# A fixed order at the tokenizer's end, Wv transposed earlier, and gathers that wait for an earlier unit

## The chip, the cores and the metric

The kernel runs on one core of a Trainium2 chip. A core has five engines with instruction streams of their own: TensorE (PE; its weight loads are listed as PEld), VectorE (DVE), ScalarE (ACT), GpSimd (POOL) and SyncE (SP). Each executes its stream in order and meets the others at semaphores. Transfers go through 16 DMA engines; they are issued by SP, ACT or, for gathers and scatters by a list of rows, by GpSimd. The metric is the device time of one execution, in microseconds. All data are 32-bit floats.

## The reference

Four images of 3 x 224 x 224 go through a tower of two layers:

- The tokenizer cuts each image into 28 x 28 = 784 patches of 8 x 8 x 3 = 192 numbers, normalises each, multiplies by W1 (to 256), normalises, multiplies by Wp1, normalises, applies SiLU and multiplies by Wp2. The reference repeats the tokens three times (`concatenate([q, k, tokens])`); the kernel computes them once (3136 rows of 256 in all) and writes the result three times.
- Layer 0: h is normalised twice (once ahead of the block, once in it), projected to queries, keys, values and a gate; the attention is over the four images, not over the tokens; then Wo, and h is added. After it a mixture of 6 experts of three matrices each, the best two per row.
- Layer 1: a linear attention (`qkv = x @ W_qkv`; q and k centred and squared, with k^T v per image), then Wout, and h added; after it a shared network and 4 small experts, the best two per row.

## The kernel before

Rows are handled in 28 tiles of 112, seven to an image. Up to the experts of layer 0 and in the last stage they go in 7 groups of 4 tiles (`groups`, `GT = 4`); in layer 1's attention in 8 units, two to an image, of 4 and 3 tiles (`units`, L1400).

The framework derives semaphores from the tiles that each instruction reads and writes. Inside `tc.manual_schedule(engines=...)` the named engines keep the order of the program; elsewhere a planner sets the order of each engine by its own modelled times. Either way, an engine that waits holds up all that stands behind it in its stream.

**Tokenizer (L506 to L573).** `first_rows(g)` multiplies a group's patches (`pw`, L515), takes statistics (L519), the root (L523) and its reciprocal, scales and adds (`y`, L528), takes statistics again (L531), a second root (L534) and writes the normalised rows `xn` (L538). `turned_rows` transposes them on PE and applies SiLU on ACT (L548). The last part multiplies by Wp2 (`pwp`) and adds into `h` (L566). `tokenize(g)` does the first part of group g, the second of g-1 and the third of g-2; the loop over g = 0 to 6 is in the planner's hands.

**Keys and values (L1049 to L1104), written out by hand.** `second_norm(g)` and `second_rows(g)` normalise h twice (statistics L236, roots L239 and L245, rows L1060). `keys_values(g)` transposes the rows, applies gamma and beta (`mT`, L1070), and multiplies by Wk and Wv (`pkv`, copied at L1079); the normalisation of group g+1 stands in between. The leftover parts of the tokenizer, `tokenize(7)` and `tokenize(8)`, stand around `keys_values(0)`:

```python
second_rows(0, second_norm(0))
tokenize(len(groups))
keys_values(0)
tokenize(len(groups) + 1)
for g in range(1, len(groups)):
    keys_values(g)
```

**Zero fill (L468 to L481).** Two tables in HBM, `xrows` and `yrows`, of 20224 rows each, are filled with zeros from the tile `nothing`, by SP, once `cols` is there. The experts' input rows are scattered into `xrows` (L950) and their results land in `yrows` (L1250).

**Experts of layer 0 (L1257 to L1512).** 30 blocks of 256 rows. At their end `fetch(u)` (L1411) gathers a unit's two result rows per token, by two indirect DMAs per tile (L1420) into `ys`, of which there are three; `fetch(0)`, `fetch(1)` and `fetch(2)` stand here, each behind the blocks that may hold its rows.

**Layer 1's attention (L1599 to L1805), in the planner's hands.** For a unit u: `stats_one` adds the gathered rows into h with their weights (L1434) and takes statistics; `normalise` writes `xa` (L1457); `x_t` transposes; `q_k` multiplies to q and k (`pqk`, L1625), adds the bias on DVE (L1629), squares and sums on ACT (L1633, L1634), and calls `stats_one` of unit u+1; `scales` makes the reciprocals and `uk` (L1657, ACT), `fold` sums. For each image `k_x` (`pukx`, L1699), `g_t` and `kv_out` make a matrix from `uk`, and `rows_out` writes h. `layer1_weights`, in unit 1, transposes Wv (L647), copies it (L651), multiplies by Wout (`pwvo`, L656). `fetch(3)` is called at the head of unit 0, and `fetch(u + 3)` at the head of each later unit:

```python
if u == 0:
    fetch(3)
    x_t(1)
    q_k(0, 0, GT)
```

Of the kernel before, what the change touches and what calls it, by code (L numbers as in the profile page):

```python
# [60 lines left out]
def tile_vit_tower(ctx: ExitStack, tc: tile.TileContext, a: dict, out: bass.AP):  # L61
# [230 lines left out]
    def halves(tiles):  # L292
        return [tiles[i : i + 2] for i in range(0, len(tiles), 2)]
# [3 lines left out]
    def cut(t0, n):  # L297
        return slice(t0 * TT, (t0 + n) * TT)
# [168 lines left out]

    nothing = tokp.tile([P, 8 * D], F32, tag="nothing", name="nothing")  # L468
    nc.gpsimd.memset(nothing, 0.0)
    for r in range(0, XROWS, 8 * P):  # L470
        n = min(8, (XROWS - r) // P)
        for rows_ in (xrows, yrows):
            put = nc.sync.dma_start(
                out=rows_[r : r + n * P, :].rearrange("(p k) d -> p (k d)", k=n),
                in_=nothing[:, : n * D],
            )
            tc.add_manual_dep(
                put.ins, turned.ins.name,
                mybir.DependencyInfo(mybir.DependencyClass.Sync, mybir.DependencyReason.DATA),
                reason="later",  # L480
            )  # L481
# [23 lines left out]

    def first_rows(g):  # L506

        t0 = groups[g][0]
# [14 lines left out]
        nc.scalar.activation(r, r, AF.Sqrt, bias=zero[:TT])  # L523
        nc.vector.reciprocal(r, r)
        st = small.tile([TT, GT, 6], F32, tag="st", name="st")
        mv = small.tile([TT, GT, 2], F32, tag="mv", name="mv")
        for j in range(GT):
            nc.vector.scalar_tensor_tensor(  # L528
                y[:, j, :], y[:, j, :], r[:, j : j + 1], bp1, ALU.mult, ALU.add
            )  # L530
            nc.vector.bn_stats(st[:, j, :], y[:, j, :])  # L531
            nc.vector.bn_aggr(mv[:, j, :], st[:, j, :])
        r = small.tile([TT, GT], F32, tag="rstd", name="rstd")
        nc.scalar.activation(r, mv[:, :, 1], AF.Sqrt, bias=eps[:TT])  # L534
        nc.vector.reciprocal(r, r)
        xn = tokw.tile([TT, GT, D], F32, tag="xn", name="xn")
        for j in range(GT):
# [3 lines left out]
            )  # L541
        return xn

# [13 lines left out]
    def tokenize(g):  # L557
        if g < len(groups):
            normed[g] = first_rows(g)
        if 1 <= g <= len(groups):  # L560
            third[g - 1] = turned_rows(normed.pop(g - 1))
        if g >= 2:
            sT = third.pop(g - 2)
            t2 = groups[g - 2][0]
            for two in halves(range(GT)):
                nc.vector.tensor_tensor(  # L566
                    h[:, t2 + two[0] : t2 + two[0] + 2, :],
                    mm_rows(two, lambda c, j: sT[:, c, cut(j, 1)], Wp2, "pwp2"),
                    over(bp2, 2), ALU.add,
                )  # L570
    for g in range(len(groups)):
        tokenize(g)
    tok.close()  # L573
    tcol = const.tile([NQ, 4], F32, tag="tcol", name="tcol")
# [66 lines left out]

    def layer1_weights():
        WvT = w1p.tile([P, 2, D], F32, tag="WvT", name="WvT")
        pt = ps_tile("pwv").rearrange("p (k i) -> p k i", k=2)
        for k in range(2):
            for c in range(2):
# [3 lines left out]
                )  # L650
        nc.vector.tensor_copy(WvT, pt)  # L651
        Wvo = w1p.tile([P, 2, D], F32, tag="Wvo", name="Wvo")
        for c in range(2):
# [36 lines left out]
    nc.vector.tensor_scalar(bgh, col2("bg"), 0.5, None, ALU.mult)  # L690
    ENG = mybir.EngineType
    by_hand = {ENG.DVE, ENG.PE, ENG.Activation}
    qTs, gates, atts, oTs, sums, rows0, turned0, logits0, picked, mixed = ({} for _ in range(10))
# [354 lines left out]

    xns = {}  # L1049

    def second_norm(g):
        t0 = groups[g][0]
        return ln_stats(lambda j: h[:, t0 + j, :], GT, twice=True)

    def second_rows(g, stats):
        mv, r = stats
        t0 = groups[g][0]
        xn = xns[g] = tokw.tile([TT, GT, D], F32, tag="xn", name="xn")
        for j in range(GT):
            nc.vector.tensor_scalar(  # L1060
                xn[:, j, :], h[:, t0 + j, :], mv[:, j, 0:1], r[:, j : j + 1],
                ALU.subtract, ALU.mult,
            )

    def keys_values(g):
        t0 = groups[g][0]
        at = cut(t0, GT)

        def put(c, pt):
            nc.scalar.activation(  # L1070
                mT[:, c, at], pt, AF.Identity, scale=col("gamma", c), bias=col("beta", c)
            )

        transposed(xns.pop(g), GT, put)
        if g + 1 < len(groups):
            stats = second_norm(g + 1)
        for w, dst in ((Wk, kT), (Wv, vT)):
            for o in range(2):
                nc.scalar.copy(  # L1079
                    dst[:, o, at],  # L1080
                    mm_t(GN, w, slice(o * P, (o + 1) * P), lambda c: mT[:, c, at], "pkv"),
                )
            if dst is kT and g + 1 < len(groups):
                second_rows(g + 1, stats)

        ht = h[:, t0 : t0 + GT, :]
        nc.vector.tensor_tensor(ht, ht, over(bo, GT), ALU.add)

    with tc.manual_schedule(engines=by_hand):
        second_rows(0, second_norm(0))  # L1090
        tokenize(len(groups))
        keys_values(0)
        tokenize(len(groups) + 1)
        for g in range(1, len(groups)):
            keys_values(g)

            if g == 1:
                for o in range(2):
                    q_mm(0, o)
                    q_copy(0, o)  # L1100
            t, rest = divmod((g + 1) * GT, TPI)
            if rest < GT and g + 1 < len(groups):
                for o in range(2):
                    products(0, o, [t - 1])  # L1104
# [306 lines left out]
    def fetch(u):  # L1411
# [5 lines left out]
        for j in range(n):  # L1417
            for k in range(2):
# [4 lines left out]
                )  # L1423
                tc.add_to_no_dep_group("fetched", got.ins)

    lw = []

# [214 lines left out]
    def scales(u):  # L1642
# [13 lines left out]
        for j in range(n):  # L1656
            nc.scalar.activation(uk[:, j, :], qk[:, j, D:], AF.Copy, scale=ss[:, j, 1:2])  # L1657
            nc.vector.tensor_scalar(
                qk[:, j, :D], qk[:, j, :D], ss[:, j, 0:1], None, ALU.mult
            )  # L1660
        for j in range(n):
            nc.scalar.activation(sq[:, j, :], uk[:, j, :], AF.Square)
# [93 lines left out]
    for u in range(len(units) + 2):  # L1756
        b, odd = divmod(u - 2, 2)
        one_image = u >= 2 and not odd
        if u == 0:
            fetch(3)  # L1760
            x_t(1)
            q_k(0, 0, GT)
            squares[0] = scales(0)
            fold(0, squares.pop(0))
            continue
        if u < len(units):
            fetch(u + 3)
        if u == len(units):
# [13 lines left out]
        if u < len(units):  # L1782
            q_k(u, 2, GT)
            if u == 1:
                lw.extend(layer1_weights())
                Wvo, bvo = lw[:2]
            squares[u] = scales(u)
        if one_image and b:
            kv_out(b, gT)
# [113 lines left out]
```

## Time and profile before

| | |
|---|---|
| median of 4 runs | 824.34 us (822.27 to 830.22) |
| profiled execution | 821.9 us, its span 820.0 us, mean granted clock 0.952 |
| PE busy | 738.7 us, 90% |
| DVE busy | 501.3 us, 61% |
| ACT busy | 333.6 us, 41% |
| POOL busy | 131.9 us, 16% |
| DMA | 97.38 MB; about 420 GB/s from 40 to 130 us, under 330 after that |

The profile is of one execution; times count from its first instruction. A row of the timeline gives start, duration, engine, line, operation, what is written from what is read, and how many; in brackets the engine's idle time before it, and what ended it. "issue" means that nothing the profile shows was waited for, "remote" that a semaphore ended the wait whose raising the profile can't put down to an instruction. A row x16 is 16 records; PE shows two records for each multiplication of 32-bit floats. In the page's slices each digit is a tenth of a slice (20.5 us). "PEclk" is the granted clock of PE in tenths of full speed. Matrix tiles in PSUM have names with p (`pqk`), numbers at a name's end are left out.

From the timeline, layer 1's units begin (first `pqk`) at 489.6, 496.4, 556.9, 564.8, 584.1, 600.6, 619.9 and 636.4 us.

### The profile page before, as it was taken

Reading aid. Unit: us, or ns where it says so; the run is one execution under the profiler, and the core shown is the slowest. Engines: PE = TensorE matmul, PEld = TensorE weight load, DVE = VectorE, ACT = ScalarE, POOL = GpSimd, SP = SyncE. Lnnn points to the kernel's source line nnn. Section 1 sums busy time; section 2 is a strip of 40 time slices with the busy share of each in tenths; the row PEclk is TensorE's granted clock in tenths of the full one; section 3 lists DMA queues with packets and bytes.
Section 4 is the critical chain, followed back from the end, with each engine's and each line's share of the span. In section 5 each row is a group of like instructions: output and inputs, shape, how many; then the busy total and the mean of one; then the engine's idle time right before and its main releaser. Section 6 shows DMA issues by size and latency. Waiting matters only on the chain. (4 is left out here: it accounts for less than half of the span.)

```text
span 820.0 us, 10856 instructions
## 1 busy us (share of the span) xinstructions
PE 738.7 (90%) x3516; PEld 501.1 (61%) x3516; DVE 501.3 (61%) x1549; ACT 333.6 (41%) x789; POOL 131.9 (16%) x219
## 2 busy tenths in 40 slices
PE   6899969999898787999999996189999999999996
PEld 4755545556565565888888873165777675555553
DVE  4677765769778743355447565179994745554441
ACT  0557754455574651432223225026554503222221
POOL 5200000000165236300120206542000000000000
PEclk9999979999999887999999998679999999999998
DMA  8499996000021944332342343211000003333333
GB/s 199 128 420 417 421 419 265 1 1 0 6 73 46 321 143 128 113 100 92 97 132 86 117 119 91 79 48 31 1 1 1 1 4 77 103 94 94 92 95 93
DMA packets 58182, 97.38 MB, mean 119 GB/s; under 512 B 14519, under 2 KB 48494, under 8 KB 53262
## 3 DMA queue, kind: packets, MB, share of 16 engines
q1 hardware_dynamic: 50832, 80.52, 28.4%
q0 software_dynamic: 6112, 14.01, 5.9%
q10 hardware_dynamic: 1182, 2.16, 1.1%
q8 instruction: 28, 0.46, 0.2%
q14 instruction: 28, 0.23, 0.1%
HBM read 30.93 MB, written 65.74 MB: 118 GB/s over the span
## 5 line engine op out<-in xcount | busy, mean ns | idle before, releaser
L950 POOL DMA_INDIRECT xrows<-xn,pos x56 | 59.6, 1064 | 255.2 <-ACT kq L714 206.5
L1420 POOL DMA_INDIRECT ys<-yrows,pos x56 | 54.5, 974 | 161.2 <-DMA yrows<-yb 132.4
L1224 PE MATMUL pb<-xTb,own 128*128 128x256 f32 x240 | 59.6, 393 | 5.9 <-issue 2.3
L1241 PE MATMUL pyb<-own,hb 128*128 128x256 f32 x240 | 58.7, 387 | 3.8 <-ACT hb L1230 3.8
L1230 ACT ACTIVATE hb<-pb,own 128x256 f32<-128x256 f32 x74 | 34.8, 474 | 61.1 <-PE pb L1224 40.6
L1224 PE MATMUL pb<-hb,own 128*128 128x256 f32 x240 | 58.8, 389 | 0.3 <-DVE hb L1232 0.3
L1224 PEld LDWEIGHTS pb<-xTb,own 128*128 128x128 f32 x240 | 45.3, 197 | 15.5 <-issue 4.2
L1241 PEld LDWEIGHTS pyb<-own,hb 128*128 128x128 f32 x240 | 46.0, 193 | 11.3 <-ACT hb L1230 5.0
L1625 PE MATMUL pqk<-Wqkv,lxT 128*112 128x512 f32 x112 | 49.7, 594 | 0.5 <-ACT lxT L81 0.5
L515 PE MATMUL pw<-Wall,pT 128*112 128x512 f32 x112 | 49.3, 593 | 0.0
L1224 PEld LDWEIGHTS pb<-hb,own 128*128 128x128 f32 x240 | 44.5, 195 | 6.3 <-DVE hb L1232 0.9
L1214 ACT COPY xTb<-ptb 128x512 f32<-128x512 f32 x30 | 17.5, 584 | 71.9 <-PE ptb L1210 59.5
L1247 DVE TENSOR_TENSOR yb<-pyb,eb 128x512 f32<-128x512 f32 x30 | 20.7, 691 | 41.9 <-PE pyb L1241 35.7
L1699 PE MATMUL pukx<-xa,uk 112*128 112x258 f32 x112 | 28.6, 411 | 18.7 <-ACT uk L1657 18.7
L264 PE MATMUL pt<-ident,xn 112*128 112x112 f32 x224 | 35.1, 291 | 11.2 <-DVE xn L538 6.6
L273 PE MATMUL pe<-xT,eW 128*128 128x448 f32 x112 | 45.2, 546 | 0.0
L264 PEld LDWEIGHTS pt<-ident,xn 112*128 112x128 f32 x224 | 27.5, 154 | 25.2 <-issue 8.8
L1232 DVE TENSOR_SCALAR hb<-pb,own 128x256 f32<-128x256 f32 x46 | 22.1, 481 | 31.4 <-PE pb L1224 27.6
L1699 PEld LDWEIGHTS pukx<-xa,uk 112*128 112x128 f32 x112 | 22.4, 206 | 22.4 <-issue 19.1
L515 PEld LDWEIGHTS pw<-Wall,pT 128*112 128x112 f32 x112 | 19.6, 177 | 25.1 <-issue 21.4
L739 DVE SCALAR_TENSOR_TENSOR prod<-kq 128x784 f32<-128x784 f32 x32 | 30.3, 969 | 7.1 <-ACT kq L714 5.2
L1625 PEld LDWEIGHTS pqk<-Wqkv,lxT 128*112 128x112 f32 x112 | 19.3, 177 | 24.8 <-issue 23.0
(361 smaller groups left out, 1497.2 us busy)
## 6 DMA issues: line engine op xcount, KB each, us to landing
xrows<-nothing SPq DMA_DIRECT2D x19, 1024.0 KB, 19.6
yrows<-nothing SPq DMA_DIRECT2D x19, 1024.0 KB
out_dram<-h SPq DMA_DIRECT2D x26, 336.0 KB, 3.8
xb<-xrows SPq DMA_DIRECT2D x30, 256.0 KB, 2.7
yrows<-yb SPq DMA_DIRECT2D x30, 256.0 KB, 2.1
ew<-in_L_ffn_expert_w_dram SPq DMA_DIRECT2D x6, 768.0 KB, 11.8
wb<-wd SPq DMA_DIRECT2D x28, 112.0 KB, 3.0
img<-in_x_dram SPq DMA_DIRECT2D x2, 588.0 KB
```

Source lines behind the costliest of these rows:

```text
L264: nc.tensor.transpose(pt[:, j * TT : (j + 1) * TT], xn[:, j, c * P : (c + 1) * P], ident[:TT, :TT])
L273: nc.tensor.matmul(pm[: wcols.stop - wcols.start, :n], w[:, c, wcols], xT(c), start=(c == 0), stop=(c == chunks - 1),)
L515: nc.tensor.matmul(pm, pTf[:, c, cut(t0 + j, 1)], Wall[:, c, :], start=(c == 0), stop=(c == 1))
L739: nc.vector.scalar_tensor_tensor(prod, qTs[s][:, o, :], 1.0, kT[:, o, t * SEQ : (t + 1) * SEQ], ALU.mult, ALU.mult, accum_out=atts[s][:, o ...
L950: put = nc.gpsimd.indirect_dma_start(out=xrows[:, :], out_offset=bass.IndirectOffsetOnAxis(ap=pos[:, k, t0 + j : t0 + j + 1], axis=0), in_ ...
L1224: nc.tensor.matmul(pm, wm[:, c, o * P : (o + 1) * P], src[:, c, :], start=(c == 0), stop=(c == 1),)
L1230: nc.scalar.activation(dst[:, o, :], pm, AF.Relu, bias=b)
L1232: nc.vector.tensor_scalar(dst[:, o, :], pm, b, 0.0, ALU.add, ALU.max)
L1241: nc.tensor.matmul(pm[:, t, :], src[:, c, t * P : (t + 1) * P], wm[:, c, :], start=(c == 0), stop=(c == 1),)
L1420: got = nc.gpsimd.indirect_dma_start(out=y[:, j, k, :], out_offset=None, in_=yrows[:, :], in_offset=bass.IndirectOffsetOnAxis(ap=pos[:, k, ...
L1625: nc.tensor.matmul(pqk, xT[:, c, cut(j, 1)], Wqkv[:, c, : 2 * D], start=(c == 0), stop=(c == 1),)
L1699: nc.tensor.matmul(pg, uks[u][:, k, c * P : (c + 1) * P], xas[u % 4][:, k, : D + 2], start=(j == 0), stop=(j == TPI - 1),)
```

## The change

Four edits:

1. In the tokenizer, `first_rows` is cut into three steps (`first_steps`, a generator). The loop ends with group 5; the last group is written out by hand, its three steps with the turning of group 5 and the last part of group 4 between them. The second normalisation of group 0 is moved ahead of group 5. In the keys, each group's transposes go one group ahead (`turn_second(g + 1)` between Wk and Wv of g) and its normalisation two groups ahead; `xn` gets three buffers, and the tokenizer's remaining parts stand inside `keys_values(0)`.
2. The zero tile `nothing` is 7 rows wide in place of 8, so the fill has 23 DMAs for each table in place of 20.
3. The transposes of Wv and their copy (`turn_wv`) are called in unit 0, ahead of its `pqk`, in place of unit 1.
4. `fetch(3)` is taken out of unit 0, and each unit calls `fetch(u + 2)` behind `scales(u)` in place of `fetch(u + 3)` at its head. From unit 3 on each gather waits for the last `uk` of the unit two before.

```diff
-    nothing = tokp.tile([P, 8 * D], F32, tag="nothing", name="nothing")
+    nothing = tokp.tile([P, 7 * D], F32, tag="nothing", name="nothing")
...
-    for r in range(0, XROWS, 8 * P):
-        n = min(8, (XROWS - r) // P)
+    for r in range(0, XROWS, 7 * P):
+        n = min(7, (XROWS - r) // P)
...
     def first_rows(g):
+        for _ in first_steps(g):
+            pass
+
+    def first_steps(g):
...
         nc.vector.reciprocal(r, r)
+        yield
         st = small.tile([TT, GT, 6], F32, tag="st", name="st")
...
             nc.vector.bn_aggr(mv[:, j, :], st[:, j, :])
+        yield
         r = small.tile([TT, GT], F32, tag="rstd", name="rstd")
...
-    for g in range(len(groups)):
+    n = len(groups)
+    for g in range(n - 1):
+        if g == n - 2:
+            second_rows(0, second_norm(0))
         tokenize(g)
+    ENG = mybir.EngineType
+    by_hand = {ENG.DVE, ENG.PE, ENG.Activation}
+    with tc.manual_schedule(engines=by_hand):
+        steps = first_steps(n - 1)
+        next(steps)
+        third[n - 2] = turned_rows(normed.pop(n - 2))
+        next(steps)
+        last_rows(n - 3)
+        for _ in steps:
+            pass
     tok.close()
...
+    def keys_values(g):
+        projected(g, Wk, kT)
+        if g + 2 < len(groups):
+            stats = second_norm(g + 2)
+        if g == 0:
+            third[n - 1] = turned_rows(normed.pop(n - 1))
+        turn_second(g + 1)
+        projected(g, Wv, vT)
+        if g == 0:
+            last_rows(n - 1)
+        if g + 2 < len(groups):
+            second_rows(g + 2, stats)
...
     with tc.manual_schedule(engines=by_hand):
-        second_rows(0, second_norm(0))
-        tokenize(len(groups))
+        turn_second(0)
+        last_rows(n - 2)
+        second_rows(1, second_norm(1))
         keys_values(0)
-        tokenize(len(groups) + 1)
         for g in range(1, len(groups)):
             keys_values(g)
...
                 tc.add_to_no_dep_group("fetched", got.ins)
+                if u >= 3:
+                    tc.add_manual_dep(
+                        got.ins, scaled[u - 2],
+                        mybir.DependencyInfo(
+                            mybir.DependencyClass.Sync, mybir.DependencyReason.DATA
+                        ),
+                        reason="paced",
+                    )
...
         for j in range(n):
-            nc.scalar.activation(uk[:, j, :], qk[:, j, D:], AF.Copy, scale=ss[:, j, 1:2])
+            got = nc.scalar.activation(uk[:, j, :], qk[:, j, D:], AF.Copy, scale=ss[:, j, 1:2])
...
+        scaled[u] = got.ins.name
...
         if u == 0:
-            fetch(3)
             x_t(1)
+            WvT = turn_wv()
             q_k(0, 0, GT)
...
-        if u < len(units):
-            fetch(u + 3)
...
             if u == 1:
-                lw.extend(layer1_weights())
+                lw.extend(layer1_weights(WvT))
                 Wvo, bvo = lw[:2]
             squares[u] = scales(u)
+            fetch(u + 2)
```

`last_rows(g)` is the third part of `tokenize`, `turn_second(g)` the transposes and `mT` of `keys_values`, and `projected(g, w, dst)` one of its two products, each with its code unchanged. In the tokenizer and in `second_rows` the tile `xn` is asked for with `bufs=3`.

## The prediction

> **What bounds the kernel now.** I read the slices of the page first, for where TensorE (PE) is not full.
>
> ```profile
> ## 2 busy tenths in 40 slices
> PE   6899969999898787999999996189999999999996
> ...
> DVE  4677765769778743355447565179994745554441
> ...
> PEclk9999979999999887999999998679999999999998
> ```
>
> A slice is 20.5 us. From slice 27 (about 555 us) on PE is full to the end, so whatever brings that point forward shortens the kernel. Before it, two slices stand out that the change touches: slice 5 (102 to 123, the tokenizer's end) and slices 24 to 26 (492 to 553, the border of the layers), where DVE, ACT and PE are all low in slice 25. Next I read PE's timeline for the first hole:
>
> ```profile
> 101.96 0.59 PE L284 MATMUL pwp<-Wp,xTt 128*112 128x256 f32 x2
> 102.39 0.74 PE L264 MATMUL pt<-ident,xn 112*128 112x112 f32 x6
> 102.97 3.19 PE L284 MATMUL pwp<-Wp,xTt 128*112 128x256 f32 x14
> ...
> 112.97 2.08 PE L264 MATMUL pt<-ident,xn 112*128 112x112 f32 x8 [6.57 <-DVE xn L538]
> 114.83 5.88 PE L284 MATMUL pwp<-Wp,xTt 128*112 128x256 f32 x16
> 120.55 0.93 PE L264 MATMUL pt<-ident,xn 112*128 112x112 f32 x8
> 121.92 3.27 PE L273 MATMUL pkv<-mT,Wk 128*128 128x448 f32 x8 [0.43 <-ACT mT L1070]
> ```
>
> PE waits 6.57 us for the last group's normalised rows, and then runs at half speed: eight transposes take 2.08 us, where the same eight take 0.93 at 120.55; the granted clock is 0.50 from 110 to 115. Then the waits of the second hole (who waited, for whom, us, times, longest):
>
> ```profile
> PE pukx L1699 <- ACT uk L1657: 18.7, 1, 18.7
> ...
> ACT lqT L81 <- remote: 11.1, 1, 11.1
> DVE ss L1648 <- remote: 8.5, 1, 8.5
> ...
> ACT junk L1634 <- remote: 6.0, 2, 4.3
> DVE lqT L83 <- remote: 5.9, 1, 5.9
> ACT s L1649 <- remote: 5.6, 1, 5.6
> ```
>
> "remote" is a semaphore raised late by nothing that the profile shows. DVE's `ss` at 517.77 needed ACT's sum that ended at 515.5 at the latest; `lqT` at 533.21 needed PE transposes that ended at 513.8. Last, GpSimd's timeline for what runs beside it:
>
> ```profile
> 493.98 0.92 POOL L1420 DMA_INDIRECT ys<-yrows,pos  x1 [22.19 <-DMA yrows<-yb]
> 495.21 0.93 POOL L1420 DMA_INDIRECT ys<-yrows,pos  x1 [0.30 <-issue]
> ...
> 527.65 0.93 POOL L1420 DMA_INDIRECT ys<-yrows,pos  x1 [0.30 <-issue]
> 537.67 0.92 POOL L1420 DMA_INDIRECT ys<-yrows,pos  x1 [9.09 <-DVE h L1434]
> ```
>
> 28 gathers run back to back from 494.0 to 528.6 (units 2 to 5, one each 1.24 us). All late semaphores of the kernel lie in such runs or just behind them: up to 2.1 us behind the 8 gathers ending at 417.2, 7.3 us in the 14 scatters of 297.8 to 315.5, and 509 to 533 here. Two runs of 14 scatters, at 1.42 and 1.44 us each, and five of 6 or 8 show none. I take the run of gathers as the cause; that it is one is inferred.
>
> **The change, part by part.** Times are against the profiled execution: 821.9 us, span 820.0 and 1.9 around it. The median of the runs shown, 824.34, is 2.4 above.
>
> *Paced gathers.* `fetch(3)` leaves unit 0 and comes after `scales(1)`; each later `fetch(u)` waits for the last `uk` of unit u-2. GpSimd has only gathers queued there, so the wait holds up nothing else. The run of 28 ends after 8, at 503.8, before the first late semaphore (509). Without these ACT goes on: its last square of unit 1 starts at 509.0 in place of 514.98 (without the 1.6 waited at 509.34 and the 4.3 ahead of it) and ends at 509.6. In unit 0 it took 2.0 from there (501.58) to the first `uk` (503.59), so unit 1's `uk` starts at 511.6. Before it started at 533.64 and unit 2's first `pqk` at 556.9, 23.3 later. I keep the 23.3 (PE waits some 4 us for `uk` then too, so its slow clock stays): `pqk` of unit 2 at 534.9, **22.0 us earlier**; 0 if the semaphores stay late.
>
> What is late next: the gathers. Unit 2's `uk` took 12.8 us from its first `pqk`, so ends at 547.7. `fetch(4)` takes 8 x 1.24 = 9.9, its last pair is used 2.65 after issue (493.98 to 496.63), less 0.9 of issue already counted: 11.7. Then two multiply-adds, statistics and mean (1.5), root, reciprocal and four rows (2.5), eight transposes and a copy (1.5): `pqk` of unit 4 at 564.9. Before it came 27.2 behind unit 2's (584.1 and 556.9), so at 562.1: **2.8 us lost**. From unit 4 to unit 6 `pqk` takes 35.8 now and the chain 12.8 + 17.2 = 30, so nothing is lost; the 3-tile units have four gathers' time more. Bounds: 0, if PE has other rows to fill the wait, to 11.5, if DVE waits in order (second rival).
>
> *Wv's transposes.* 8 PE records (0.60 us) and one DVE copy (0.68) move from unit 1 to unit 0. PE waited 6.34 us for that copy, but beside the wait for `uk`; the path is through `uk`, so I count 0. In unit 0 they stand ahead of `pqk`: at most +1.3 if nothing hides them, and -1 if `pwvo` fills the gap well.
>
> *Tokenizer's end.* Nothing is removed; order moves. On ACT the root of the last group (L523, table load 1.28 and 0.30) stood behind half of the Silu of the group before, so it ran at 106.35, though its input was ready at 103.2; by hand it goes first, at 104.6. DVE's chain then runs 1.7 us earlier, and loses the four h-statistics (110.1 to 112.2) that stood ahead of L535: rows of group 6 end at 111.5, not 113.8. Meanwhile PE has `pwp` of group 4 (to 106.3), group 0's transposes (0.93), `pwp` of group 5 (3.45, from 107.7 when Silu is done) and Wk of group 0 (3.0), to 114.2: the idle 6.57 and some 3.9 of half speed (2.08 - 0.93, 5.88 - 3.2) are filled. What is late next is DVE: h of group 5 (1.4), statistics of group 1 (2.3), two roots there and back (2.0), rows (1.4): second transposes at 118.5, a PE gap of 3.4. Then ACT's two Silu with a table load hold `pwp` of group 6 to 125. So Wk of group 1 starts at 128.5 (132.85 now), and behind the queries, where the 0.43 and wait for the transposes go, Wk of group 2 at 140.8 (145.6): 4.8 earlier. Second_norm(0) moves into the full tokenizer loop: 4.6 us of DVE work against 2.8 idle in each 11.1 us period, so I charge 1.3 (0 to 3, with table loads). Groups 3 to 6 go from 7.53 to about 7.0 each (0.48 wait): 2.0. **5.5 us earlier**; from +1 (the gap grows by what DVE is late) to -10 (all idle and half speed gone).
>
> The Trainium skill, "TensorE: Matmul & The Clock Gate", on the HAM clock gate, says that PE falls to half clock after an idle window of about 3.4 us and needs as long a busy one to recover. The row agrees: 0.50 behind 6.57 us. By it the gap of 3.4 that I leave could cost a further 1.7 us, an estimate that the sum leaves out.
>
> *Zero fill.* 46 DMAs of at most 896 KB in place of 40: 6 more issues of 0.33 us on SP, behind which nothing waits; the fill ends about 140 and the first scatter is at 222.7. 0, as is the third `xn` buffer (space).
>
> Sum: 821.9 - 22.0 + 2.8 - 5.5 = 797.2, and 2.4 more for the median: **about 800 us**.
>
> **The rivals.**
> 1. *The stall comes back in smaller runs.* Unit 3's `uk` comes 7.2 us behind unit 2's (569.7, 576.9), less than `fetch(4)` takes, so units 4 and 5 make one run of 14; 6 and 7 perhaps too. One of three runs of 14 cost 7.3. For: its pace, 1.29, was nearest to the gathers'. Against: the next gathers now, at 1.27 and 1.34, show none. 7 to 14 us back: 807 to 814. Chance 0.16.
> 2. *DVE waits in order for the gathers.* If `h<-ys` stands ahead of the next unit's adds, each `uk` waits for a gather that waits for the `uk` before: 20 us for 4 tiles and 17 for 3, 74 from unit 2 to unit 6, against 62.5 now (569.7 to 632.2). 11.5 in place of 2.8: about 808. For: DVE waited 2.73 so at 493.9. Chance 0.12.
> 3. *Slower: the semaphores are late for another reason at this place.* Then nothing is won, and the wait is pure cost at each unit: 11.5 at worst, with a tokenizer that gives between 0 and 5.5: 830 to 836. It decides when less than 6 of the 22 us go. For: two runs of 14 showed no late semaphore. Chance 0.09.
> 4. *The change does nothing for the second hole:* the stall stays and the wait is hidden: 819 to 824, by the tokenizer alone. Chance 0.09.
>
> **How the numbers follow.** My forecast (no stall, small pacing loss) has 0.54: 789 to 806. A measurement of this kernel tells about 1% from no change, that is 816 to 833. Faster by over 1%: 0.54, 0.16 and 0.12, less 0.01: 0.81. Within 1%: rival 4 and the edges, 0.11. Slower: 0.08. The range runs from 787 (824.3 - 22.0 - 10, and 4.8 of half speed gone between `uk` and `pqk`: 16 `pukx` in 6.17 for 3.50, 8 `pkvo` in 3.06 for 1.73, 4 `pout` in 1.69 for 0.87) to 823, which leaves out rival 3 and a little on either side.
>
> **What would show it.** GpSimd's gathers in runs of 8 and 6 from 494 on; no "remote" wait after 500, `uk` of unit 1 near 506 (511.6 less 5.5), and PE's wait for it about 4 us, not 18.7; `pqk` of unit 2 some 27 earlier than 556.9. If gathers are split and the "remote" waits stay, rival 3 or 4 holds; if "DMA ys" ends DVE's idle time in units 3 to 6, rival 2. At the tokenizer: no PE wait for `xn` L538, a shorter one for group 1's rows, Wk of group 2 near 140.8. Wrong would also be a planner that, outside the hand-written blocks, orders the units otherwise.

## The result, and the profile after

The changed kernel took 820.92 us (median of 42 runs, 816.56 to 826.88), the kernel before, run beside it, 826.21 (63 runs, 820.45 to 836.88): a ratio of 0.9941, 95% interval 0.9925 to 0.9956. It is faster by 0.6%, where 3% were forecast. The profiled execution has a span of 813.8 us (820.0 before) and a mean granted clock of 0.963.

The experiments ran on five chips. On two of them the kernel before takes 788 us, not 826 to 831, and no trace taken there has a single wait that ends "remote". I call them chips without late semaphores; the result above is from the other kind. Ratios are always to the kernel before on the same chip.

The slices of the page after (busy tenths; the last line is TensorE's granted clock):

```profile
## 2 busy tenths in 40 slices
PE   7899989998987887899999998758979999999996
...
DVE  4677785867978743464457478557479745554441
...
PEclk9999999999999887999999999987999999999999
```

The two holes of before are mostly filled: slice 5 (102 to 122 us) and slice 25 (509 to 529), where PE had 6 and 1 tenths and now has 8 and 7. New ones stand behind the second: slices 26, 27 and 29 (529 to 570 and 590 to 610) with 5, 8 and 7, where 8, 9 and 9 stood. GpSimd's timeline shows the pacing, and the chain of waits (who waits, for whom: us in all, times, longest) what came of it:

```profile
487.14 0.92 POOL L1458 DMA_INDIRECT ys<-yrows,pos  x1 [21.93 <-DMA yrows<-yb]
...
507.06 0.92 POOL L1458 DMA_INDIRECT ys<-yrows,pos  x1 [10.36 <-DVE qk L1705]
...
538.41 0.92 POOL L1458 DMA_INDIRECT ys<-yrows,pos  x1 [24.03 <-ACT uk L1704]
...
553.24 2.47 POOL L1458 DMA_INDIRECT ys<-yrows,pos  x1 [4.77 <-DVE xa L1504]
```

```profile
POOL ys L1458 <- ACT uk L1704: 54.7, 3, 24.0
...
DVE h L1481 <- DMA ys<-yrows,pos: 19.4, 28, 1.9
...
PE pt L264 <- DVE xa L1504: 18.3, 2, 12.8
```

The run of 28 gathers is now runs of 8, 6, 8, 6, 8 and 6. No wait behind 470 us ends "remote" any more, and `uk` of unit 1 starts at 505.48 where it started at 533.64. In their place GpSimd waits 24.0 us for `uk` of unit 2, DVE waits 28 times for a gather, and PE waits 12.8 us, and once more 5.5 (18.3 less 12.8), for normalised rows. PE's timeline has the place (start, duration, and in brackets the idle time before):

```profile
526.45 7.12 PE L1672 MATMUL pqk<-Wqkv,lxT 128*112 128x512 f32 x16 [0.24 <-ACT lxT L81]
533.40 0.74 PE L264 MATMUL pt<-ident,xa 112*128 112x112 f32 x6
534.39 5.40 PE L1672 MATMUL pqk<-Wqkv,lxT 128*112 128x512 f32 x12 [0.24 <-ACT lxT L81]
552.61 1.98 PE L264 MATMUL pt<-ident,xa 112*128 112x112 f32 x8 [12.82 <-DVE xa L1504]
554.38 1.91 PE L1788 MATMUL pout<-Wvo,lxT 128*112 128x256 f32 x4
...
560.18 1.03 PE L1788 MATMUL pout<-Wvo,lxT 128*112 128x256 f32 x4
...
563.06 6.34 PE L1747 MATMUL pukx<-xa,uk 112*128 112x258 f32 x28
569.23 0.74 PE L264 MATMUL pt<-ident,qk 112*128 112x112 f32 x6
569.81 3.60 PE L1672 MATMUL pqk<-Wqkv,lxT 128*112 128x512 f32 x8
```

Unit 2 begins 30.5 us earlier than before (526.4 for 556.9). Unit 4 begins 43.4 us behind it (27.2 before), unit 6 42.7 behind unit 4 (35.8): 23.1 us of the 30.5 are given back, and what stays is about the 7.3 us that the tokenizer won, the size by which the first scatter (215.4 for 222.7) and the first gather (399.7 for 407.0) come earlier. Behind unit 6 another 1.1 us go (201.3 to the end, 200.2 before), so the spans differ by 6.2 us; the medians differ by 5.3.

### The profile page after: what moved, and what is told of

Same layout as the page of the kernel before. It is cut to its first block, busy times and chain, and to the rows that moved or that the text cites. A ratio compares the mean times of both kernels' runs of the same rounds, so it can differ in the third digit from the quotient of the medians.

```text
span 813.8 us, 10858 instructions
## 1 busy us (share of the span) xinstructions
PE 737.9 (91%) x3516; PEld 499.4 (61%) x3516; DVE 503.6 (62%) x1549; ACT 329.9 (41%) x787; POOL 132.7 (16%) x219
## 4 chain that ended last, share of the span: by engine, by line
PE 68%; DVE 13%; ACT 7%; DMA 3%; issue 3%; POOL 2%; another core or an unknown queue 1%; SPq 0%; DVEq 0%; POOLq 0%; ACTq 0%
PE pb L1262 12%; PE pyb L1279 6%; PE pe L273 5%; PE pw L519 5%; PE pkv L273 4%; PE ps L273 4%; PE pt L264 4%; PE ps L1904 3%; PE pwp L284 3%; PE pout L1788 3%; PE pout L1793 2%; PE pqk L1672 2%; POOL ys L1458 2%; DMA ys<-yrows,pos 2%; DVE oT L815 2%
## 5 line engine op out<-in xcount | busy, mean ns | idle before, releaser
L1481 DVE SCALAR_TENSOR_TENSOR h<-ys,wk,h 112x256 f32<-112x256 f32 x56 | 26.8, 480 | 19.7 <-DMA ys<-yrows,pos 19.4
L1680 ACT ACTIVATE qk<-qk 112x256 f32<-112x256 f32 x56 | 22.7, 406 | 28.9 <-DVE qk L1676 16.5
```

What stands on the lines that cost most here:

```text
L1481: nc.vector.scalar_tensor_tensor(h[:, t, :], ys[u][:, j, k, :], wk[:, k, t : t + 1], h[:, t, :], ALU.mult, ALU.add,)
```

## The experiments

All kernels are the changed kernel with the edit shown, unless another is named. The table counts from one unit's first `pqk` to another's, in the profiled execution, which leaves out the stretch ahead of the units.

| kernel | ratio, 95% interval | 1 to 2 | 2 to 4 | 4 to 6 | 1 to 6 |
|---|---|---|---|---|---|
| *late semaphores:* | | | | | |
| before | 1 | 60.5 | 27.2 | 35.8 | 123.4 |
| changed | 0.9941 (0.9925-0.9956) | 36.0 | 43.4 | 42.7 | 122.0 |
| tokenizer_only | 0.9924 (0.9888-0.9959) | 62.6 | 27.8 | 35.7 | 126.0 |
| tokenizer_only_2 | 0.9968 (0.9927-1.0008) | 62.8 | 27.2 | 35.7 | 125.6 |
| change_2 | 0.9951 (0.9909-0.9993) | 36.9 | 42.0 | 43.6 | 122.5 |
| change_3 | 0.9941 (0.9905-0.9978) | 38.7 | 42.3 | 43.7 | 124.7 |
| pacing_only | 1.0004 (0.9967-1.0041) | 37.0 | 43.3 | 44.3 | 124.6 |
| by_turn | 0.9892 (0.9856-0.9929) | 38.7 | 42.1 | 42.8 | 123.7 |
| rows_first | 0.9867 (0.9816-0.9918) | 37.0 | 37.0 | 40.6 | 114.6 |
| alternating_2 | 0.9839 (0.9771-0.9906) | 37.1 | 37.4 | 43.8 | 118.4 |
| alternating_rows_2 | 0.9828 (0.9758-0.9899) | 39.3 | 30.8 | 44.1 | 114.2 |
| runs_of_8_2 | 0.9783 (0.9723-0.9843) | 34.6 | 31.2 | 41.3 | 107.0 |
| spaced_3 | 1.0332 (1.0256-1.0409) | 43.8 | 53.2 | 59.5 | 156.5 |
| *none late:* | | | | | |
| tokenizer_alone | 0.9912 (0.9886-0.9939) | 36.9 | 27.2 | 35.8 | 99.9 |
| wv_back | 1.0245 (1.0202-1.0288) | 39.4 | 43.4 | 42.6 | 125.3 |
| alternating | 1.0129 (1.0096-1.0162) | 37.3 | 38.1 | 38.5 | 113.9 |
| alternating_rows | 1.0061 (1.0042-1.0080) | 35.5 | 29.7 | 40.9 | 106.0 |
| runs_of_8 | 1.0074 (1.0047-1.0101) | 37.3 | 30.8 | 40.6 | 108.7 |
| spaced, spaced_2 | 1.0624 (1.0599-1.0649), 1.0613 (1.0576-1.0649) | 43.4 | 53.0 | 59.3 | 155.7 |

(The last row's stretches are those of spaced_2.)

**Which part does what: tokenizer_only, pacing_only.** First the change with its pacing undone:

```diff
-                if u >= 3:
-                    tc.add_manual_dep(got.ins, scaled[u - 2], ..., reason="paced")
...
-            x_t(1)
+            fetch(3), x_t(1)
...
+        fetch(u + 3 if u < len(units) else 99)
...
-            fetch(u + 2)
```

> The changed kernel with its pacing undone: unit 3 fetched at the start of unit 0, unit u+3 at the start of unit u, no wait on the scaled keys; the tokenizer's new end and the early transposes of Wv stay. Theory (a long run of gathers makes semaphores late; the paced gathers then come too late, which gives all of that back; what is left of the change is the tokenizer's 7 us): the first scatter at 215 as in the changed kernel, 28 gathers in a row again, the first unit-2 pqk about 60 us behind the first unit-1 pqk (before: 60.5; after: 35.9), and a time within 0.3% of the changed kernel's, 819 to 823 against 826 of the kernel before. Rival A (the early transposes of Wv, not the pacing, took the stall away): no stall, first unit-2 pqk about 37 us behind that of unit 1, a time of 798 to 805. Rival B (the pacing is worth its share and the tokenizer's gain was lost further down): 824 to 828.

It took 823.1 us, the kernel before 830.62. 28 gathers in a row are back, and so is the stall, with Wv's transposes in their early place. Its chain of waits:

```profile
DVE bvo L711 <- remote: 16.8, 1, 16.8
...
ACT junk L1681 <- remote: 9.8, 2, 6.8
...
DVE lqT L83 <- remote: 6.9, 1, 6.9
...
ACT lqT L81 <- remote: 6.2, 1, 6.2
```

Rival A is out. Then the pacing alone, put into the kernel before (the same lines, added):

> The kernel before with the paced gathers alone: gathers of unit u wait for the last scaled keys of unit u-2, called after the scales of unit u-2; tokenizer and Wv as before. Theory: no wait for a semaphore of the long run, unit-2 pqk at 533 to 536 instead of 556.9, then TensorE waits 11 to 14 us for the rows of unit 4 and 5 to 6 us for those of unit 6, and the end is where it was: ratio to the kernel before 0.997 to 1.003, some 824 to 828. Rival A (Wv's early place did it): stall still there, pqk of unit 2 near 557. Rival C (the pacing is worth 20 us and the changed kernel lost them through something else that it moves): 803 to 808.

830.67 us, beside 830.62. No "remote" wait in the units, and the stretches 37.0, 43.3 and 44.3 are those of the changed kernel. So the pacing takes away 23.5 us of stall (60.5 to 37.0) and puts 24.6 us in its place (16.1 and 8.5 more between units 2 and 4 and units 4 and 6): nothing is left of it, with or without the other edits.

**Gathers released earlier: by_turn.** Units 4 to 7 wait for the copy of the transposed rows of unit u-2, some 10 us ahead of its `uk`:

```diff
-                        got.ins, scaled[u - 2],
+                        got.ins, scaled[1] if u == 3 else xc[u - 2].ins.name,
```

> The changed kernel with the gathers of units 4 to 7 released earlier: not by the last scaled keys of unit u-2 but by the second copy of its transposed rows, ahead of its pqk (unit 2: 527.4 to 528.0 instead of 538.1); unit 3 stays paced by the keys of unit 1. Theory (lateness of the gathers gave the gain back): gathers of unit 4 start at 528 to 529 instead of 538.4, the 12.8 us wait for the rows of unit 4 shrinks to under 4, the later one likewise; 8 to 20 us faster than the changed kernel, 800 to 812. Rival D (semaphores of runs of 14 or 22 gathers are late again, as unit 5 now follows unit 4 with no pause): unit 2's or 3's squares and adds stall by 6 us or more and the time is 815 to 825. Rival E (the order in which the planner set the rows of unit 4 on TensorE, not the lateness, made the wait): 818 to 823.

It took 822.33 us. The kernel before took 830.62 on this chip, 826.21 in the result above, so the ratio is the fairer measure: 0.9892 lies in rival D's range (815 to 825 of 826.21, 0.986 to 0.999) and just outside rival E's (818 to 823, 0.990 to 0.996), though its interval reaches into that. Rival D's sign, a late semaphore in units 2 or 3, is in the trace, though shorter than its 6 us. Unit 4's gathers start 1.8 us behind unit 2's first `pqk` (12.0 in the changed kernel), but unit 5's follow with no pause. GpSimd's timeline, and DVE's:

```profile
538.80 0.92 POOL L1458 DMA_INDIRECT ys<-yrows,pos  x1 [16.36 <-DVE lxT L83]
...
554.81 0.93 POOL L1458 DMA_INDIRECT ys<-yrows,pos  x1 [0.31 <-issue]
```

```profile
541.46 0.48 DVE L1481 SCALAR_TENSOR_TENSOR h<-ys,wk,h 112x256 f32<-112x256 f32 x1
542.78 0.48 DVE L1481 SCALAR_TENSOR_TENSOR h<-ys,wk,h 112x256 f32<-112x256 f32 x1 [0.84 <-DMA ys<-yrows,pos]
...
557.88 0.69 DVE L1676 TENSOR_TENSOR qk<-pqk,bqkv 112x512 f32<-112x512 f32 x1 [4.29 <-remote]
```

14.8 us into the run DVE's add of unit 3 begins to wait for a late semaphore, 4.29 us, until 2.1 us behind the run's end; ACT waits 1.95 the same way. Ahead of it DVE's adds of unit 2 stand behind multiply-adds that wait for gathers just issued (0.84 here). The rows of unit 4 are done as far behind unit 2's `pqk` as in the change (25.5 and 25.7 us).

**TensorE's order: rows_first.**

```diff
-        if 2 <= u < len(units) - 1:
-            x_t(u + 1)
...
         if u >= 2 and (b or odd):
             rows_out(u - 2)
+        if 2 <= u < len(units) - 1:
+            x_t(u + 1)
```

> The changed kernel with the outputs of unit u-2 written ahead of the transposes of unit u+1 in the program, so that TensorE has three pairs of pout ahead of the wait for unit 4's rows and four ahead of that for unit 6's; gathers paced as in the change. Theory: the rows of unit 4 come no earlier (first transposes at about 552 to 553), but 5 to 7 us of pout leave the stretch behind it, so that unit 4's pqk is at 563 to 565 instead of 569.8; some 3 to 5 us more at unit 6; 810 to 816. Rival E (order alone): the whole wait is filled, 800 to 806. Rival F (what TensorE waits for next, the scaled keys of unit 3 behind the same VectorE queue, ends no earlier): 819 to 822.

818.92 us: the rows of unit 4 come no earlier (26.2 us behind unit 2's `pqk`), but 37.0 for 43.4 and 40.6 for 42.7 us pass between the units, and 2.0 are lost behind unit 6 (203.3 to the end, for 201.3). As the theory had it, part of the wait is filled by work that stood behind it: PE waits 8.16 us for unit 4's rows, for 12.82. The ratio, 0.9867, is that of the 810 to 816 expected (0.980 to 0.988 of 826.21). It is 0.7% lower than the change's, with an interval that just misses that of the result above; it does meet the wider ones of change_2 and change_3, and the change did not run on this chip.

**Both prices apart: alternating, alternating_rows, runs_of_8.** The first price is the late semaphores beside a long run of gathers, the second the late rows where gathers are held back. Units 4 and 6 are released by the transposed rows, 3, 5 and 7 by `uk`; the second and third kernel have the order of rows_first too, and the third releases unit 6 by the copy of gT of image 1.

```diff
-                        got.ins, scaled[u - 2],
+                        got.ins, scaled[u - 2] if u % 2 else xc[u - 2].ins.name,
```

> The changed kernel with the gathers of units 4 and 6 released by the copies of the transposed rows of units 2 and 4 (as in the run before), and those of units 3, 5 and 7 by the last scaled keys of units 1, 3 and 5 (as in the change), so that no run is longer than 8 gathers and each has a pause behind it. Theory of two prices (late gathers on one side, runs of more than about 12 gathers on the other: in the run before, VectorE's add waited 4.3 us for a late semaphore 15 us into the 14 gathers of units 4 and 5): no late semaphore, gathers of unit 4 about 1 to 2 us behind the first pqk of unit 2, rows of unit 4 normalised about 20 us behind that pqk (changed kernel 25.7, run before 25.6), 6 to 12 us faster than the changed kernel: 809 to 815. Rival D' (the late semaphore comes whatever the run's length): rows of unit 4 again 25 us behind, 820 to 823. Rival G (the gathers' pace is no matter at all, VectorE's own order is): 817 to 823.

> The same, with the outputs of unit u-2 ahead of the transposes of unit u+1 as in the run before. If the two repair different things, both gains add up to some 10 to 18 us against the changed kernel: 803 to 811. If they repair the same wait, the sum is no better than the better of the two: 809 to 816.

These two fell on a chip without late semaphores: 796.3 and 791.96 us beside 787.57. With only the second price there, they are 1.3 and 0.6% slower than the kernel before, where the change with Wv's transposes put back (wv_back, below) is 2.45% slower. Their second runs fell on the other kind:

> The kernel with runs of at most 8 gathers, those of units 4 and 6 released by the transposed rows of units 2 and 4. Where semaphores come late: no wait for one behind 490 us, 6 to 12 us faster than the changed kernel beside it, ratio to before 0.980 to 0.988. Where they don't: slower than before by 1.0 to 1.6%, as in the run before.

> The same with the outputs of unit u-2 ahead of the transposes of unit u+1. Where semaphores come late: 10 to 18 us faster than the changed kernel, ratio to before 0.972 to 0.982. Where they don't: 1.004 to 1.008 of the kernel before, as in the run before.

They took 813.95 and 813.49 us, beside 826.29 for the kernel before and 819.86 for the change. The ratios are as the theory of two prices had them, the second just past its slow edge, but both are only some 6 us faster than the change, where 6 to 12 and 10 to 18 were expected, and "no late semaphore" was wrong: units 5 and 6 had made a run of 14, and 12.4 us into it (6.00 us of waiting by DVE) or 17 us (2.4) they were there. The third kernel takes that run apart:

```diff
+                        got.ins, scaled[u - 2] if u % 2 else (xc[2] if u == 4 else xc["gT"]).ins.name,
...
-        nc.scalar.copy(gT, pt)
+        xc["gT"] = nc.scalar.copy(gT, pt)
```

> As the last run with outputs ahead of the transposes, but the gathers of unit 6 released by the copy of gT of image 1, some 4 us behind the first pqk of unit 4: in that run they followed those of unit 5 with no pause, 14 gathers in 17.5 us, and VectorE waited 2.4 us for a late semaphore (6.0 us in its sister run). Where semaphores come late: none behind 490 us, 3 to 8 us faster than that run's 0.983 of before: 0.973 to 0.980. Where they don't: 1.000 to 1.010 of before.

> Runs of at most 8 gathers with pauses, and outputs ahead of the transposes; so far 1.0074 of before where no semaphore comes late. Where they come late: no wait for one behind 490 us, 0.973 to 0.980 of before, 12 us and more faster than the changed kernel beside it. Where they don't: 1.005 to 1.010 again.

The first fell on a chip without late semaphores again (793.27 beside 788.58). On the other kind: 810.44 us, beside 829.74 and the change's 824.87, 14.4 us less. Its GpSimd timeline, the first gathers of units 4, 5 and 6:

```profile
535.31 0.92 POOL L1458 DMA_INDIRECT ys<-yrows,pos  x1 [12.34 <-DVE lxT L83]
...
559.70 0.92 POOL L1458 DMA_INDIRECT ys<-yrows,pos  x1 [14.87 <-ACT uk L1704]
...
572.30 0.92 POOL L1458 DMA_INDIRECT ys<-yrows,pos  x1 [5.28 <-ACT gT L1764]
```

With pauses of 12.3, 14.9 and 5.3 us the late waits of the units come down to one of 0.5 us. Both prices can be cut together; 31.2 and 41.3 us between the units, for 27.2 and 35.8 unpaced, say that some 9.5 us of the second are still paid.

**Rate or number: spaced.** The unpaced gathers, with eight fills of a scratch tile by GpSimd behind each of them from unit 2 on (the edit is shortened here).

```diff
+                for _ in range(8 if u >= 2 else 0):
+                    got = nc.gpsimd.memset(pad, 0.0)   # each ordered behind the one before
```

> The changed kernel with the pacing undone (as in the first run), but eight small fills of a scratch tile on GpSimd behind every gather from unit 2 on, about 1.2 us together, so that the gathers of units 2 to 5 are issued 2.4 us apart instead of 1.24. If the rate makes the semaphores late: no late semaphore, scaled keys of unit 1 about 15 us behind the first pqk of that unit (with the run of gathers: 40), first pqk of unit 2 about 37 behind, and 800 to 815, less what late rows of units 4 and 5 cost. If it is the number of gathers without a pause: the stall comes back once some 12 are out, 28 us into the run, about 523 to 565: 820 to 845. If GpSimd's own work beside ACT and VectorE is what makes them late: stall as before.

> The 28 gathers of units 2 to 5 in a row, 2.4 us apart, on a chip where semaphores come late (it may be given to either kind; where they don't, it can only repeat the 1.06 of its first run). If the rate counts: no wait for a late semaphore behind 490 us, scaled keys of unit 1 about 20 us behind its first pqk and no more. If the number without a pause counts: VectorE's or ACT's waits of 4 us and more from 25 to 30 us into the run. Either way 830 to 880, since every gather is later than VectorE asks for it.

> The gathers of units 2 to 5 issued 2.4 us apart, as before; so far on two chips where no semaphore comes late (836.8 and 836.5, the kernel before 788). Where they come late: if the rate counts, no late semaphore behind 490 us and 1.02 to 1.04 of before (the same 836 to 850, the kernel before 826 to 831); if the number without a pause counts, waits of 4 us and more from 25 to 30 us into the run and 850 to 880. Where they don't: 836 again.

The first two fell on chips without late semaphores (836.8 and 836.5 us) and tell nothing of them. The third, on the other kind, took 857.22 us beside 829.74: 1.033, what the rate's theory gave. The pace in GpSimd's timeline is 3.14 us where nothing is waited for (3.34 in the mean), not 2.4:

```profile
490.69 0.92 POOL L1471 DMA_INDIRECT ys<-yrows,pos  x1 [21.98 <-DMA yrows<-yb]
491.61 2.05 POOL L1479 MEMSET pad<- 128x128 f32 x8
493.82 0.94 POOL L1471 DMA_INDIRECT ys<-yrows,pos  x1 [0.15 <-issue]
```

42 gathers follow one another from 490.7 to 628.6, GpSimd never idle for more than 1.7 us, and no wait in that stretch ends "remote". From unit 1 to unit 6 it takes 156.5 us, and 155.7 on the other kind of chip: at this pace the two hardly differ. So, by this one trace, it is the gathers' rate that makes semaphores late, not their number or GpSimd's being busy. What it costs instead is the second price, without any pacing. DVE's waits behind 470 us:

```profile
DVE h L1501 <- DMA ys<-yrows,pos: 61.4, 36, 4.0
```

**The tokenizer and Wv: tokenizer_alone, wv_back.** The first is tokenizer_only with this edit, the second the changed kernel with it:

```diff
-            WvT = turn_wv()
...
-                lw.extend(layer1_weights(WvT))
+                lw.extend(layer1_weights(turn_wv()))
```

> The kernel before with the tokenizer's new end alone (and its zero fill): Wv's transposes in unit 1, gathers as before. Where semaphores come late: the stall in unit 1 as before, 0.990 to 0.997 of before (with Wv early it was 0.9924 and 0.9968). Where they don't: 28 gathers in a row with no stall, 0.988 to 0.994 of before, some 780. If Wv's early place is worth anything without the pacing, the ratio is more than 0.3% from those two.

On a chip without late semaphores: 781.28 us beside 788.58. GpSimd issues 42 gathers in a row, the first and the last of them:

```profile
474.75 0.92 POOL L1458 DMA_INDIRECT ys<-yrows,pos  x1 [21.76 <-DMA yrows<-yb]
...
528.43 0.93 POOL L1458 DMA_INDIRECT ys<-yrows,pos  x1 [0.30 <-issue]
```

Nothing is late; from unit 1 to unit 6 it takes 99.9 us. Set beside tokenizer_only_2, which differs in Wv's place only but ran on the other kind of chip (spans 820.4 and 778.2), the 42.2 us between them lie ahead of the first gather (11.5), from there to unit 1 (5.0) and from unit 1 to unit 2 (25.9); from there to the end the two agree within 0.1 us at each step.

> The changed kernel with Wv's four transposes back behind the pqk of unit 1, where the kernel before has them; the rest as in the change. They are 1 us of TensorE either way, and TensorE waits for the scaled keys of unit 1 behind them: theory, no difference that can be measured, 819 to 823. Rival (their early place delays the first pqk or, late, they delay Wvo's product and with it the first outputs): 2 us either way.

It fell on a chip without late semaphores too, 807.13 us beside 787.57, and so tells more of the pacing than of Wv: there the wait costs 23.0 us (43.4 and 42.6 less 27.2 and 35.8), buys nothing, and the kernel is 2.45% slower. The changed kernel itself did not run on that kind. Wv's place has no pair of kernels of its own: on chips of this kind it is 125.2 and 127.6 us from the first gather to unit 2's `pqk` with Wv late (tokenizer_alone, wv_back), and 124.2 to 126.0 with Wv early (alternating, alternating_rows, runs_of_8), in kernels that differ in other things too.

The two repeats beside these, of the change with its pacing undone and of the change itself:

> The first run's kernel (the change with its pacing undone) once more, beside the changed kernel itself. So far the kernel before took 826 to 831 us where late semaphores show in the traces (two sets of runs) and 788 us on a chip where no trace shows one. Theory: semaphores behind 12 or more gathers come late on some chips and not on others. Where they do: 28 gathers in a row, a stall of 20 to 25 us in unit 1, and within 0.3% of the changed kernel. Where they don't: the same 28 gathers in a row with no wait for a late semaphore, scaled keys of unit 1 some 15 us behind its first pqk, 778 to 784 where the kernel before has 788, and 20 to 28 us less than the changed kernel. Rival H (the quick chip is quick for another reason, its clock or its DMAs, and stalls as well): late semaphores in the trace of a kernel of 780 to 790 us.

> The changed kernel itself. Where semaphores come late: ratio to the kernel before 0.990 to 0.998, as measured. Where they don't: the pacing costs what it cost there with Wv's transposes put back (1.0245), 1.020 to 1.028 of the kernel before. Rival H: a ratio of 0.99 to 1.00 on either chip, and Wv's place cost the 3% in that run.

> The changed kernel. Where semaphores come late: 0.990 to 0.998 of before. Where they don't: 1.020 to 1.028, since there the paced gathers take some 23 us from pqk of unit 2 to pqk of unit 6 (43.3 and 42.6 us apart with pacing, 27.1 and 35.8 without) and give nothing back.

All three fell where semaphores come late: 0.9968, 0.9951 and 0.9941, with the intervals of the table. Rival H needed late semaphores in a quick trace; in the seven traces taken on the two quick chips there is none.

## Why the prediction was right or wrong

**The stall (22.0 us): right, in place and size.** Its signs came: `uk` of unit 1 at 505.48 (506), PE's wait for it 3.39 us (4), unit 2's `pqk` at 526.4 (529.4 with the tokenizer's 5.5). From unit 1 to unit 2 it takes 36.0 us for 60.5, so 24.5 for the 22.0: the 23.3 us from `uk` to `pqk`, which I kept, became 21.0. That the fast run of gathers is the cause is now shown by its return (tokenizer_only), by a shorter run elsewhere (by_turn) and by its absence at a slower pace (spaced_3). That the stall depends on the chip no view of one trace could tell.

**The gather chain (2.8 us): the step that failed.** It measured 23.1: 16.2 from unit 2 to unit 4 and 6.9 from there to unit 6. The chain itself was right: from the end of unit 2's `uk` (538.1) to the copy of unit 4's transposed rows (555.5) it took 17.4 us, for 17.2. Wrong was what I let follow. PE's timeline before, from the products of unit 3 to those of unit 4:

```profile
564.84 5.40 PE L1625 MATMUL pqk<-Wqkv,lxT 128*112 128x512 f32 x12 [0.24 <-ACT lxT L81]
570.08 0.93 PE L264 MATMUL pt<-ident,xa 112*128 112x112 f32 x8
570.85 1.03 PE L1740 MATMUL pout<-Wvo,lxT 128*112 128x256 f32 x4
...
576.79 3.66 PE L1699 MATMUL pukx<-xa,uk 112*128 112x258 f32 x16
...
580.80 2.86 PE L1699 MATMUL pukx<-xa,uk 112*128 112x258 f32 x12
583.49 0.74 PE L264 MATMUL pt<-ident,qk 112*128 112x112 f32 x6
584.07 3.60 PE L1625 MATMUL pqk<-Wqkv,lxT 128*112 128x512 f32 x8
```

I set `pqk` of unit 4 at the end of that chain, as though all that stands between the units ran beside it. In PE's stream the transposes of unit 4 stand ahead of unit 1's outputs and of `pukx`, and PE waits in order: 12.82 us idle, and behind it the same outputs and `pukx` as ever, up to 569.8 (17.2 us from the transposes to `pqk`, 14.0 before). The 27.2 us of before, which I took for a limit that hides a chain of 30, were already filled with PE work; a wait inside them is added whole. The rest, 3.3 us, is the clock (below). From unit 4 to 6 I compared 35.8 with a chain of 30 and made the same mistake: 5.52 us idle at 597.16 and 1.4 of slow clock are the 6.9.

**Rival 2 (DVE waits in order): its sign came, but PE did not lose by it.** DVE's timeline after, at unit 3:

```profile
550.26 0.48 DVE L1481 SCALAR_TENSOR_TENSOR h<-ys,wk,h 112x256 f32<-112x256 f32 x1 [0.43 <-DMA ys<-yrows,pos]
550.67 0.17 DVE L1491 BATCH_NORM_AGGREGATE mv<-st 112x2 f32<-112x6 f32 x1
550.76 0.14 DVE L1695 TENSOR_SCALAR ss<-ss 112x6 f32<-112x6 f32 x1
```

ACT's root for unit 3 had run at 542.99, but `ss` stood behind eight multiply-adds that each waited for a gather, so `uk` came at 551.68, over 8 us behind that root, and GpSimd, done with unit 4's gathers at 548.5, began unit 5's at 553.24. From `uk` of unit 2 to that of unit 6 it takes 88.5 us (536.4 to 624.9); I had worked out 74 for this rival, with 62.5 before. But PE waited for none of this: it took up `uk` of unit 3 at 563.06, ten us after it was there, and `uk` of unit 5 and the rows of units 5 and 7 without a wait either. Its two waits are for the rows of units 4 and 6, whose chains ran as forecast (17.4 us, and 17.8 from the end of unit 4's `uk` at 582.1 to 599.9). Rival 2 left out PE's order as the forecast did.

**Rivals 1, 3 and 4.** Runs of 14 did not arise in the change itself, because each `uk` waits for the gathers before it; in by_turn and alternating_2 they did, at 4 to 6 us each, for the 7 of rival 1 (2.4 in alternating_rows_2). Rival 3 named the right balance, but its point of decision lies with the chip: where no semaphore is late, nothing can be won and the wait is pure cost (wv_back: 2.45%). Rival 4's time came (819 to 824) by another way: not a stall that stays, but a stall taken away and given back.

**The tokenizer (5.5 us): right, a little small.** 7.3 us at the first scatter, and 7.3 by itself in tokenizer_alone (781.28 for 788.58). PE's timeline after:

```profile
116.38 0.93 PE L264 MATMUL pt<-ident,xn 112*128 112x112 f32 x8
119.03 1.58 PE L264 MATMUL pt<-ident,xn 112*128 112x112 f32 x8 [1.72 <-DVE xn L593]
120.45 3.19 PE L273 MATMUL pkv<-mT,Wv 128*128 128x448 f32 x8
125.35 3.89 PE L284 MATMUL pwp<-Wp,xTt 128*112 128x256 f32 x16 [1.72 <-ACT xTt L554]
129.08 3.17 PE L273 MATMUL pkv<-mT,Wk 128*128 128x448 f32 x8
...
141.15 3.17 PE L273 MATMUL pkv<-mT,Wk 128*128 128x448 f32 x8
```

Predicted were 118.5, 125, 128.5, and 140.8 for Wk of group 2, which came at 141.15 (145.6 before). Of the 1.3 us charged for the moved normalisation at most 0.35 shows there (141.15 for 140.8), and what follows Wk of group 2, the groups 3 to 6 above all, gave 2.9 us (7.3 less 4.45), not 2.0.

**The clock.** At the tokenizer the gap of 3.4 us that I left became one of 1.72, with another of 1.72 ahead of the last `pwp`, and the granted clock stayed at 1.00. The half clock came elsewhere: the granted clock from 540 to 550 and 550 to 560 us was 0.60 and 0.54, and a row of four records of `pout` took 1.91 us there, 1.03 at full speed. The Trainium skill, "TensorE: Matmul & The Clock Gate", on the HAM clock gate, gives a budget of about 3.4 us of time for the return to full rate; here the `pout` records are 0.43 us apart from 554.4 to 558.6 and 0.22 from 559.1 on, so the return took over 6 us from the first transpose at 552.61, and cost 3.3. Behind the second wait it took about 3, near the budget, and cost 1.4 (the granted clock is 0.50 from 597 to 600):

```profile
597.16 0.61 PE L264 MATMUL pt<-ident,xa 112*128 112x112 f32 x2 [5.52 <-DVE xa L1504]
...
600.24 1.03 PE L1793 MATMUL pout<-kvo,lqT 128*112 128x256 f32 x4
```

The measurement decides: in this stretch an idle time of 12.8 us cost 3.3 on top of itself (6.71 us from 552.61 for what takes 3.4 at full speed), one of 5.5 us 1.4 (3.08 for 1.64).

**Wv and the zero fill (0): not refuted.** The kernels with Wv early and late overlap in the stretch given above; the fill was not tried alone.

## What to carry to other kernels

Before a stretch between two marks is used as cover for a new chain, look at what fills it on the engine that sets the end, and in which order: a wait put ahead of work in an in-order stream is added whole, however much time the stretch has. Where a burst of gathers disturbs other engines, break it by pauses and release each part as early as its buffers allow, not by the end of the work just before it is needed. And take a time from more than one chip before a wait is added against a stall that only some chips have.

## What the runs showed of the hardware

- Where semaphores come late, they do so in and just behind runs of gathers or scatters 1.2 to 1.3 us apart, and not in a run 3.14 us apart, nor behind the two runs of 14 scatters at 1.42 and 1.43 us each that lie between 215 and 274 us in all 13 traces from such chips. On the other kind 42 gathers in a row at 1.31 us each (54.6 us in all) delay nothing. Which part of the chip makes the difference stays open.
- The length from which it begins isn't settled, and the "12 or more gathers" of the expectations holds in the units only. There it took 12 to 17 us of a run, and runs of 8 and 6 show waits of 0.5 us at most. But at the layers' border runs of 8 or 6 are enough: in each of the 13 traces a wait beside or just behind them (405 to 480 us) ends "remote". In runs_of_8_2 DVE waited 3.72 us, until 415.08, for a product that PE had ended at 411.0, beside 8 gathers issued from 403.6 to 413.5. In the changed kernel itself DVE read at 466.36 a product that PE had ended at 464.75, beside 6 gathers issued from 457.8 to 465.2:

```profile
466.36 0.48 DVE L1270 TENSOR_SCALAR hb<-pb,own 128x256 f32<-128x256 f32 x1 [3.15 <-remote]
```

- The half clock lasted 6 us after an idle time of 12.8 us and 3 us after one of 5.5, as worked out above.
